# The first pass of a two-layer convolution kernel: image and weights loaded first, the convolutions' tables made later and spread by SyncE, the next image's norm over three units

## The chip, the cores and the metric

The kernel runs on one core of a Trainium2 chip. A core has five engines that work beside one another, each through its own queue in order: TensorE (PE, with its weight loads shown as PEld), VectorE (DVE), ScalarE (ACT), GpSimd (POOL) and SyncE (SP). Transfers are issued by SP, ACT and POOL and run on 16 DMA engines that the core's queues share. The metric is the device time of one execution in microseconds. The time before is the median of three runs, 6082.88 us (6082.45 to 6088.8).

## What is computed

Eight images of 96 x 96 pixels with 192 channels go through two layers; each adds a branch to its input.

```python
# layer 0
x = x + conv0(groupnorm(x))
#   conv0: proj  = x @ W_in + b_in                  (192 -> 384 channels)
#          local = depthwise 3x3 of proj
#          mixed = 0.25 * (four running averages of local) + local
#          out   = layernorm(mixed) @ W_out + b_out (384 -> 192)
# layer 1
x = x + conv1(groupnorm(x))
#   conv1: depthwise 7x7, layernorm, 192 -> 768, gelu, 768 -> 192, * gamma

def groupnorm(v, G=32, eps=1e-5):      # statistics over an image's pixels
    g = v.reshape(B, H, W, G, C // G)  # and the 6 channels of a group
    m = mean(g, axis=(1, 2, 4)); s = var(g, axis=(1, 2, 4))
    return ((g - m) / sqrt(s + eps)).reshape(v.shape)
```

What matters here: the norm of an image needs all its pixels before the first of them can be projected.

## The kernel before

The kernel has five passes, A to E, joined by tensors in DRAM. **A** normalises and projects the image (192 to 384 channels) and stores the result transposed, as `P_d`. **B** reads `P_d` and makes the 3x3 convolution and the running averages with matmuls against banded tables. **C** does the layer norm and the second projection, **D** the 7x7 convolution, **E** the two dense layers. The change touches A and what stands ahead of it.

**Pass A.** An image is cut into 12 units of 8 columns (`WA = 8`, `n_t = 12`), so there are 96 units; unit `u` is unit `t = u % 12` of image `b = u // 12`. Three units make a tile `xq` of 1.77 MB, which three DMAs on SP load (`load_a(n, j)`, L323); six tiles can be held. Tile `n + 6` takes the place of tile `n`; one of its three pieces is asked for in each of the units `3n + 2`, `3n + 3`, `3n + 4`. Within a unit:

- `project_full` (L375): PE multiplies the unit's transposed pixels `xT` by two of the three parts of the weights `win`, into six PSUM banks `pm`.
- `turn_next(0)`, `turn_next(2)` (L361): PE transposes two thirds of the next unit into PSUM tiles `pt`, and ACT writes them to the next `xT` with the norm's factor and shift applied (L368).
- `project_rest` (L388): the third part of the weights; ACT (L401) and DVE (L399) then empty the six banks into `po`.
- `turn_next(1)`: the last third of the next unit, which DVE normalises (L366).
- after each third unit, `store_a` (L408, L421): POOL issues the stores of `po` to `P_d`.

PSUM has two slots for everything that carries the tag `pt`: the transposes and also the small results of the norm.

**The norm of the next image** runs beside this. `stats_a` makes 128 small steps for DVE, 32 channel groups for each of four tiles (`bn_stats`, L330); `share` says how many of them each unit takes, half before the turns and half after. The closing steps are `means` (L49 to L52), `squares` (L57 to L71), `powers` and `shift` (L75 to L79, one power on POOL), `spread` (a matmul, L342) and `keep` (DVE, L352), whose result `cols` the next image's transposes need. They are taken one after another by `end(1)`, `end(1)`, `end(2)` in unit 10 and by `end(1)`, `end(1)` in unit 11. The first image's norm has no unit to hide behind: its statistics and closing steps are written ahead of the loop.

**The convolutions' tables.** Passes B and D multiply by banded matrices that lie in DRAM as `ZB_d` and `Z2_d`. They are made from the small kernels `conv_w` and `dw_kernel`: a loaded copy (`k0`, `k1`), spread over zeros into `z0` and `z1` (L227 to L255; `k1` goes through two PE transposes `kps`, L244), and stored as `Z0_d` and `Z1_d` (L233, L261). From there DRAM-to-DRAM copies lay out shifted rows: three copies of 3.3 MB into `Z2_d` (L269), three of 1.5 MB into `ZB_d` in runs of 128 B (L445) and four small ones for its edges (L455). A zeroed `pad` goes to one row of `X1_d` (L272). The 27 copies that fill `mix` (L211), pass B's mixing matrix, stand ahead of them.

All of this up to L272 is ordered by the compiler and stands at the program's start in a block whose memory is released before pass A's tiles are laid out. The copies of L269 and L272 are issued by ACT, which also loads `win` and the bias (L300, L303). The ones to `ZB_d` are issued by ACT within the loop: `rest_steps` lists 12 stores of zeros to the edges of `P_d` (L434, POOL) and then these seven copies, and from unit 5 on each unit takes one step.

Some small loads and constants of pass C (`wo`, `gb`, `bo`, `mean_w`, `lnb`, L778 to L791) have no predecessors, and the compiler places them among these first instructions too.

Inside `manual_schedule` each engine gets its instructions in the order written.

Of the kernel before, what the change touches and what calls it, by code (L numbers as in the profile page):

```python
# [84 lines left out]
def conv_blocks_kernel(  # L85
# [31 lines left out]
    nc = tc.nc  # L117
# [98 lines left out]

    with (
        tc.tile_pool(name="zprep", bufs=1) as zp,
        tc.tile_pool(name="zpsum", bufs=1, space=PSUM) as zps,
    ):  # L220
        k0 = zp.tile([128, NC, 3, 3], F32, name="k0")
        nc.sync.dma_start(
            k0.rearrange("p m a b -> p m (a b)"),
            conv_w.rearrange("(m p) o a b -> p m (o a b)", p=128),
        )
        z0 = zp.tile([128, NC, 3, ZL], F32, name="z0")
        nc.vector.memset(z0, 0.0)  # L227
        for m in range(NC):
            nc.vector.tensor_copy(
                z0[:, m, :, RB - 1 : RB + 2],  # L230
                k0[:, m],
            )
        nc.sync.dma_start(  # L233
            Z0_d.rearrange("(m p) t l -> p m (t l)", p=128),
            z0.rearrange("p m t l -> p m (t l)"),
        )

        k1 = zp.tile([49, D], F32, name="k1")
        nc.sync.dma_start(k1, dw_kernel.rearrange("a b o c -> (a b) (o c)"))
        kps = zps.tile([128, 512], F32, name="kps")  # L240
        k1t = zp.tile([S, 2, 7, 7], F32, name="k1t")
        for i in range(2):
            half = kps[:S, i * 64 : i * 64 + 49]
            nc.tensor.transpose(half, k1[:, i * S : (i + 1) * S], ident[:49, :49])  # L244
            nc.vector.tensor_copy(k1t[:, i].rearrange("p a b -> p (a b)"), half)
        z1 = zp.tile([S, 2, PH, ZW + 64], F32, name="z1")
        nc.vector.memset(z1, 0.0)
        for i in range(2):
            for p in range(PH):
                for d in range(3):  # L250

                    kw = d * PH + p - 2
                    lo, hi = max(0, -kw), min(PH, 7 - kw)
                    if lo < hi:
                        nc.vector.tensor_copy(  # L255
                            z1[:, i, p, d * ZS + ZO : (d + 1) * ZS].rearrange(
                                "c (t e) -> c t e", e=PH
                            )[:, :, lo:hi],
                            k1t[:, i, :, kw + lo : kw + hi],
                        )  # L260
        nc.sync.dma_start(Z1_d.rearrange("(i c) p l -> c i p l", c=S), z1)  # L261
        for p in range(PH):
            n = -(-(64 - p) // PH)
            src = bass.AP(
                tensor=Z1_d.tensor,
                offset=Z1_d.offset + p * (ZW + 64),
                ap=[[PH * (ZW + 64), D], [PH, n], [1, ZW]],
            )
            nc.scalar.dma_start(Z2_d[p::PH].rearrange("r c l -> c r l"), src)  # L269
        pad = zp.tile([S, D * WV * 2 // S], F32, name="pad")  # L270
        nc.vector.memset(pad, 0.0)
        nc.scalar.dma_start(  # L272
            X1_d[BP * S * PH].rearrange("(i c) v b -> i (c v b)", i=S), pad
        )

# [13 lines left out]
    with ExitStack() as ph:  # L289
# [17 lines left out]
        for i in range(2):  # L307
# [2 lines left out]
                ident[:GROUPS, :GROUPS].unsqueeze(2).to_broadcast([GROUPS, GROUPS, GS]),  # L310
            )
        memberf = member.rearrange("p i g s -> p (i g s)")

        NK = RB // WA
        xq = {}
# [107 lines left out]
                        po[:, :, r, js[0] : js[1]].rearrange("p m j h -> p m (j h)"),  # L423
                    )

        def rest_steps():


            steps = []
            for g in range(NG):  # L430
                for m in range(NC):
                    for row, j in ((RB, 0), (RB + 1, NJ - 1)):
                        steps.append(
                            lambda g=g, m=m, row=row, j=j: nc.gpsimd.dma_start(  # L434
                                P_d[g, m * 128 : (m + 1) * 128, row, :, j], zero
                            )
                        )
            for kh in range(3):
                src = bass.AP(
                    tensor=Z0_d.tensor,  # L440
                    offset=Z0_d.offset + kh * ZL + 1,
                    ap=[[3 * ZL, C], [1, RB], [1, RB]],
                )
                steps.append(
                    lambda kh=kh, src=src: nc.scalar.dma_start(  # L445
                        ZB_d[:RB, :, kh].rearrange("r c o -> c r o"), src
                    )
                )
            for row in range(RB, RB + 4):
                src = bass.AP(  # L450
                    tensor=Z0_d.tensor,
                    offset=Z0_d.offset + (row % 2) * (RB + 1),
                    ap=[[3 * ZL, C], [ZL, 3], [1, RB]],
                )
                steps.append(lambda row=row, src=src: nc.scalar.dma_start(ZB_d[row], src))  # L455
            return steps

        n_t = S // WA
        n_x = B * NK
        rest = rest_steps()  # L460
# [853 lines left out]
```

## Time and profile before

| | before |
|---|---|
| profiled execution, device time | 6083.09 us |
| its span | 6081.0 us |
| granted PE clock, mean | 0.971 |
| PE busy | 5685.5 us, 93% |
| DVE busy | 3456.3 us, 57% |
| ACT busy | 2438.4 us, 40% |
| POOL busy | 2632.8 us, 43% |
| DMA | 1054.36 MB, 173 GB/s over the span |

The page's second part cuts the span in 40 slices of 152 us; a digit is the busy share of a slice in tenths. Pass A fills the first five and a half of them:

```profile
PE   4899989999998999999777759999999999999999
DVE  5455539999996667777632334444444444444442
PEclk9899989999999999999888879999999999999999
DMA  8987669999997888888799962222222222222221
```

The text of the prediction gives times from the start of the span, which is 2 us shorter than the device time. "POOL", "SPq" and "ACTq" with a DMA operation are rows of issuing: the time in which the engine is held by the issue, not the transfer.

### The profile page before, as it was taken

Reading aid. Unit: us, or ns where it says so; the run is one execution under the profiler, and the core shown is the slowest. Engines: PE = TensorE matmul, PEld = TensorE weight load, DVE = VectorE, ACT = ScalarE, POOL = GpSimd, SP = SyncE. Lnnn points to the kernel's source line nnn. Section 1 sums busy time; section 2 is a strip of 40 time slices with the busy share of each in tenths; the row PEclk is TensorE's granted clock in tenths of the full one; section 3 lists DMA queues with packets and bytes.
Section 4 is the critical chain, followed back from the end, with each engine's and each line's share of the span. In section 5 each row is a group of like instructions: output and inputs, shape, how many; then the busy total and the mean of one; then the engine's idle time right before and its main releaser. Section 6 shows DMA issues by size and latency. Waiting matters only on the chain.

```text
span 6081.0 us, 122820 instructions
## 1 busy us (share of the span) xinstructions
PE 5685.5 (93%) x48550; PEld 3948.3 (65%) x48550; DVE 3456.3 (57%) x8026; ACT 2438.4 (40%) x6146; POOL 2632.8 (43%) x2832
## 2 busy tenths in 40 slices
PE   4899989999998999999777759999999999999999
PEld 2455543333335989898666647777777777777777
DVE  5455539999996667777632334444444444444442
ACT  2344447777775555555433322222222222222221
POOL 0111128888886666666544433222222222322222
PEclk9899989999999999999888879999999999999999
DMA  8987669999997888888799962222222222222221
GB/s 238 230 246 238 210 191 244 245 245 242 244 244 203 253 261 267 262 265 263 230 287 286 291 167 78 63 78 62 78 62 77 63 78 63 78 63 78 63 63 37
DMA packets 570206, 1054.36 MB, mean 173 GB/s; under 512 B 109575, under 2 KB 426260, under 8 KB 567328
## 3 DMA queue, kind: packets, MB, share of 16 engines
q1 hardware_dynamic: 385312, 577.65, 35.9%
q0 software_dynamic: 124160, 450.67, 23.9%
q10 hardware_dynamic: 60160, 18.20, 1.5%
q8 instruction: 384, 6.29, 0.5%
q14 instruction: 190, 1.56, 0.1%
HBM read 585.19 MB, written 476.57 MB: 175 GB/s over the span
## 4 chain that ended last, share of the span: by engine, by line
PE 75%; DMA 7%; DVE 1%; issue 1%; POOL 1%; SPq 1%; ACT 0%; POOLq 0%; DVEq 0%; ACTq 0%
PE po L1213 19%; PE po L830 13%; PE hp L1183 12%; PE pl L576 10%; PE hp L1193 7%; PE pa L597 4%; PE pt L828 4%; DMA xin<-X_d 4%; PE pt L1166 2%; PE pa L600 2%; DMA Y_d<-yo 2%; PE py L1021 1%; DMA band<-Z_d 1%; DVE xin L1006 0%; SPq L1060 0%
## 5 line engine op out<-in xcount | busy, mean ns | idle before, releaser
L1202 ACT ACTIVATE g<-hp,b0g 128x384 f32<-128x384 f32 x1152 | 573.9, 580 | 1856.3 <-PE hp L1193 1856.3
L1213 PE MATMUL po<-w1g,g 128*128 128x192 f32 x6912 | 1178.3, 327 | 0.0
L1213 PEld LDWEIGHTS po<-w1g,g 128*128 128x128 f32 x6912 | 1116.6, 190 | 1.6 <-issue 1.1
L830 PE MATMUL po<-wc,mt 128*96 128x193 f32 x4608 | 913.3, 334 | 0.0
L1170 DVE COPY yT<-pt 128x384 f32<-128x384 f32 x288 | 251.4, 873 | 1126.9 <-PE pt L1166 1126.6
L1231 POOL DMA_DIRECT2D out_dram<-xo x576 | 321.2, 560 | 1148.0 <-DVE xo L1220 1119.5
L1183 PE MATMUL hp<-yT,w0w 128*128 128x384 f32 x2304 | 794.5, 488 | 0.4 <-ACT g L1202 0.4
L830 PEld LDWEIGHTS po<-wc,mt 128*96 128x96 f32 x4608 | 702.3, 163 | 68.4 <-ACT mean L834 65.0
L576 PE MATMUL pl<-pin,band 34*32 34x380 f32 (+1 forms) x13824 | 628.6, 489 | 18.5 <-DMA pin<-P_d 18.5
L1183 PEld LDWEIGHTS hp<-yT,w0w 128*128 128x128 f32 x2304 | 431.5, 191 | 231.5 <-issue 2.8
L606 DVE TENSOR_TENSOR_SCAN z<-decay,loc 128x768 f32<-128x768 f32 x288 | 505.8, 1756 | 59.1 <-ACT loc L585 29.3
L1021 PE MATMUL py<-xin,band 63*64 63x248 f32 (+1 forms) x6912 | 405.9, 393 | 141.6 <-DVE xin L1006 139.6
L646 POOL TENSOR_TENSOR mo<-mo,z 128x768 f32<-128x768 f32 x288 | 529.4, 1839 | 3.4 <-ACT mo L601 0.4
L615 DVE TENSOR_TENSOR_SCAN z<-decay,z 128x768 f32<-128x768 f32 x288 | 498.1, 1730 | 0.0
L576 PEld LDWEIGHTS pl<-pin,band 34*32 34x32 f32 x13824 | 233.1, 107 | 396.1 <-issue 394.8
L1021 PEld LDWEIGHTS py<-xin,band 63*64 63x64 f32 x6912 | 343.4, 142 | 203.7 <-DVE xin L1006 125.6
L837 ACT ACTIVATE sq<-pt,mean 96x384 f32<-96x384 f32 x768 | 442.9, 577 | 25.9 <-ACT mean L834 1.0
L1193 PE MATMUL hp<-yT,w0w 64*128 64x384 f32 x2304 | 449.5, 508 | 0.0
L597 PE MATMUL pa<-loc,mix 128*32 128x384 f32 x3456 | 431.9, 493 | 0.0
L600 PE MATMUL pa<-last,down 96*32 96x384 f32 x1152 | 426.8, 493 | 0.9 <-ACT mo L601 0.9
L29 POOL TENSOR_TENSOR rs<-rs_ve,neg_half 96x8 f32<-96x8 f32 x96 | 158.6, 1652 | 607.1 <-DVE rs_ve L28 607.1
L375 PE MATMUL pm<-xT,win 128*128 128x384 f32 x1152 | 401.5, 500 | 20.0 <-ACT xT L368 19.7
(116 smaller groups left out, 7712.8 us busy)
## 6 DMA issues: line engine op xcount, KB each, us to landing
P_d<-po POOLq DMA_DIRECT2D x96, 1152.0 KB, 8.8
pin<-P_d SPq DMA_DIRECT2D x192, 576.0 KB
mt<-M_d SPq DMA_DIRECT2D x576, 192.0 KB
xq<-in_x_dram SPq DMA_DIRECT2D x96, 576.0 KB
xr<-in_x_dram SPq DMA_DIRECT2D x384, 144.0 KB
X_d<-x1u POOLq DMA_DIRECT2D x192, 288.0 KB, 4.1
X_d<-x1c SPq DMA_DIRECT2D x192, 288.0 KB
y<-Y_d SPq DMA_DIRECT2D x24, 2304.0 KB
```

What stands on the lines that cost most here:

```text
L576: nc.tensor.matmul(pls[g][at * RB : (at + 1) * RB, :, lo:hi], band[rows, c, kh, :], pin[rows, c, :, NJ - 1 - j, lo + kh - 1 : hi + kh - 1] ...
L597: nc.tensor.matmul(pa[at], mix[:, i, at], loc[:, q], start=True, stop=True)
L600: nc.tensor.matmul(pa[at], down[:, to], last[:, q], start=True, stop=True)
L606: nc.vector.tensor_tensor_scan(zf, decay_f, loc.rearrange("p q n -> p (q n)"), 0.0, ALU.mult, ALU.add)
L615: nc.vector.tensor_tensor_scan(zr, decay_f, zr, 0.0, ALU.mult, ALU.add)
L646: nc.gpsimd.tensor_tensor(m, m, z, ALU.add)
L830: nc.tensor.matmul(po[:S, b], lhs[m], wc[:, m], start=(m == 0), stop=(m == NC - 1))
L1021: nc.tensor.matmul(pys[t // 2][g][k * 64 : (k + 1) * 64, t % 2, :, lo:hi], pair[k][0][rows, c, d * ZS : d * ZS + 64], pair[k][1][rows, t, ...
L1183: nc.tensor.matmul(hps[m, q], w0w[:, 2 * q, m * 128 : (m + 1) * 128], yT[:, 2 * q], start=True, stop=False,)
L1193: nc.tensor.matmul(hps[m, q], w0w[p, 1, m * 128 : (m + 1) * 128], yT[p, 1], start=False, stop=True,)
L1202: nc.scalar.activation(g[:, m, q], hps[m, q], AF.Gelu, bias=b0g[:, m : m + 1], scale=1.0)
L1213: nc.tensor.matmul(po[:, q], g[:, m, q, k * 128 : (k + 1) * 128], w1g[:, m], start=(m == 0), stop=(m == NE - 1),)
```

## The change

- **Start.** The table-making block ahead of pass A goes. SP first loads the 18 pieces of six tiles, then `k0` and `k1` (`load_kernels`). The table tiles `k0`, `k1`, `z0`, `z1`, `k1t`, `pad` now lie in a pool of pass A.
- **Tables.** In unit 3 `spread_kernels` fills `z0` and `z1`; their zeros are written by POOL instead of DVE, and `kps` takes one of the two `pt` slots. In unit 4 `store_kernels` stores `z0`, `z1` and `pad` from SP. The large copies follow from SP instead of ACT, one at a time: `Z2_d` in units 21, 33 and 45, `ZB_d` in units 57, 69 and 81, its edges in units 84 to 87. The zeros for `P_d` stay on POOL in units 5 to 16. `mix` is filled in units 17 to 19, nine copies in each.
- **Loads.** All three pieces of tile `n + 6` are asked for in unit `3n + 2`.
- **Norm.** `share` gives units 3 to 8 sixteen statistics each, so that they end with unit 8. `ends` places `means` in unit 9, `squares`, `powers` and `shift` in unit 10, `spread` and `keep` in unit 11.

In the program as built, pass C's small loads stand in SP's queue behind the three stores of `store_kernels`, and its constants `mean_w` and `lnb` in DVE's queue within units 3 and 4: `mean_w` ahead of unit 3's evictions, with a wait for the stores of `z0`, `z1` and `pad`, `lnb` ahead of unit 4's, with a wait for `gb`. ACT's table load stands behind a wait for DVE.

```diff
-    for i in range(NJ):
-        for k, (ck, jk) in enumerate(place[i]):
-            for n, (cn, jn) in enumerate(place[i]):
-                if ck == cn < CC - 1:
-                    nc.vector.tensor_copy(
-                        mix[k * RB : (k + 1) * RB, i, n * RB : (n + 1) * RB],
-                        down[jk * RB : (jk + 1) * RB, jn * RB : (jn + 1) * RB],
-                    )
-    with (
-        tc.tile_pool(name="zprep", bufs=1) as zp,
-        tc.tile_pool(name="zpsum", bufs=1, space=PSUM) as zps,
-    ):
...
-        nc.vector.memset(z0, 0.0)
...
-        for p in range(PH):
...
-            nc.scalar.dma_start(Z2_d[p::PH].rearrange("r c l -> c r l"), src)
...
+        zp = ph.enter_context(tc.tile_pool(name="zprep", bufs=1))
...
+        def load_kernels():
+            nc.sync.dma_start(
+                k0.rearrange("p m a b -> p m (a b)"),
+                conv_w.rearrange("(m p) o a b -> p m (o a b)", p=128),
+            )
+            nc.sync.dma_start(k1, dw_kernel.rearrange("a b o c -> (a b) (o c)"))
+
+        def spread_kernels():
+            nc.gpsimd.memset(z0, 0.0)
+            for m in range(NC):
+                nc.vector.tensor_copy(
+                    z0[:, m, :, RB - 1 : RB + 2],
+                    k0[:, m],
+                )
+            kps = ps_t.tile([128, 512], F32, tag="pt", name="kps")
+            for i in range(2):
+                half = kps[:S, i * 64 : i * 64 + 49]
+                nc.tensor.transpose(half, k1[:, i * S : (i + 1) * S], ident[:49, :49])
+                nc.vector.tensor_copy(k1t[:, i].rearrange("p a b -> p (a b)"), half)
+            nc.gpsimd.memset(z1, 0.0)
...
+            nc.gpsimd.memset(pad, 0.0)
+
+        def store_kernels():
+            nc.sync.dma_start(
+                Z0_d.rearrange("(m p) t l -> p m (t l)", p=128),
+                z0.rearrange("p m t l -> p m (t l)"),
+            )
+
+            nc.sync.dma_start(Z1_d.rearrange("(i c) p l -> c i p l", c=S), z1)
+            nc.sync.dma_start(
+                X1_d[BP * S * PH].rearrange("(i c) v b -> i (c v b)", i=S), pad
+            )
...
-        share = (11, 11, 10, 16, 16, 11, 11, 10, 16, 16, 0, 0)
+        rest = {3: spread_kernels, 4: store_kernels}
+        rest |= {5 + i: lambda i=i: zero_edge(i) for i in range(2 * NG * NC)}
+        rest |= {17 + i: lambda i=i: fill_mix(i) for i in range(NJ)}
+        rest |= {21 + 12 * p: lambda p=p: rows_1(p) for p in range(PH)}
+        rest |= {57 + 12 * p: lambda p=p: rows_0(p) for p in range(3)}
+        rest |= {84 + i: lambda i=i: rows_edge(i) for i in range(4)}
+
+        share = (11, 11, 10, 16, 16, 16, 16, 16, 16, 0, 0, 0)
+        ends = {(9, 0): 1, (10, 0): 1, (10, 1): 2, (11, 0): 2}
...
-            for n in range(6):
+            for n in range(NK):
                 for j in range(NJ):
                     load_a(n, j)
+            for n in range(NK, 6):
+                for j in range(NJ):
+                    load_a(n, j)
+            load_kernels()
             bn, last, cols = stats_a(0)
...
-                    if u >= 2 and n + 6 < n_x:
-                        load_a(n + 6, j)
+                    if j == 0 and n + 6 < n_x:
+                        for j in range(NJ):
+                            load_a(n + 6, j)
...
-                    if u >= 5 and rest:
-                        rest.pop(0)()
+                    if u in rest:
+                        rest[u]()
...
-                    def end(n):
-                        if more and t >= n_t - 2:
-                            for _ in range(n):
+                    def end(i):
+                        if more:
+                            for _ in range(ends.get((t, i), 0)):
                                 last.pop(0)()
...
-                    end(1)
+                    end(0)
                     ahead(share[t] // 2)
-                    if t == n_t - 1:
-                        end(1)
                     turn_next(0)
                     turn_next(2)
                     project_rest(cur, pms, po, j)
-                    if t < n_t - 1:
-                        end(1)
+                    end(1)
                     ahead(share[t] - share[t] // 2)
                     turn_next(1)
-                    if t < n_t - 1:
-                        end(2)
```

Here `rows_1`, `rows_0` and `rows_edge` are the old copies into `Z2_d` and `ZB_d` with `nc.sync` in place of `nc.scalar`, `zero_edge` is the old store of zeros, and `fill_mix(i)` is one third of the old loop over `mix`.

More of the change, by code (lines that the diff above doesn't have):

```diff
@@ L206, in conv_blocks_kernel @@
     )
-    for i in range(NJ):
-        for k, (ck, jk) in enumerate(place[i]):
-            for n, (cn, jn) in enumerate(place[i]):
-                if ck == cn < CC - 1:
-                    nc.vector.tensor_copy(
-                        mix[k * RB : (k + 1) * RB, i, n * RB : (n + 1) * RB],
-                        down[jk * RB : (jk + 1) * RB, jn * RB : (jn + 1) * RB],
-                    )
-    with (
-        tc.tile_pool(name="zprep", bufs=1) as zp,
-        tc.tile_pool(name="zpsum", bufs=1, space=PSUM) as zps,
-    ):
[L221 to L226, printed above, removed]
-        nc.vector.memset(z0, 0.0)
[L228 to L248, printed above, removed]
-            for p in range(PH):
[L250 to L268, printed above, removed]
-            nc.scalar.dma_start(Z2_d[p::PH].rearrange("r c l -> c r l"), src)
[L270 to L274, printed above, removed]
@@ L312, in conv_blocks_kernel @@
         memberf = member.rearrange("p i g s -> p (i g s)")
+        k0 = zp.tile([128, NC, 3, 3], F32, name="k0")
+        k1 = zp.tile([49, D], F32, name="k1")
+        z0 = zp.tile([128, NC, 3, ZL], F32, name="z0")
+        z1 = zp.tile([S, 2, PH, ZW + 64], F32, name="z1")
+        k1t = zp.tile([S, 2, 7, 7], F32, name="k1t")
+        pad = zp.tile([S, D * WV * 2 // S], F32, name="pad")
+        def load_kernels():
[17 more added lines that the diff above has]
+            nc.gpsimd.memset(z1, 0.0)
+            for i in range(2):
+                for p in range(PH):
+                    for d in range(3):
+                        kw = d * PH + p - 2
+                        lo, hi = max(0, -kw), min(PH, 7 - kw)
+                        if lo < hi:
+                            nc.vector.tensor_copy(
+                                z1[:, i, p, d * ZS + ZO : (d + 1) * ZS].rearrange(
+                                    "c (t e) -> c t e", e=PH
+                                )[:, :, lo:hi],
+                                k1t[:, i, :, kw + lo : kw + hi],
+                            )
[8 more added lines that the diff above has]
+                X1_d[BP * S * PH].rearrange("(i c) v b -> i (c v b)", i=S), pad
+            )
         NK = RB // WA
@@ L424, in store_a @@
                     )
[L426 to L436, printed above, removed]
-                        )
[L438 to L456, printed above, removed]
@@ new lines, in zero_edge, with fill_mix @@
+        def zero_edge(i):
+            g, m, e = i // (2 * NC), i // 2 % NC, i % 2
+            nc.gpsimd.dma_start(
+                P_d[g, m * 128 : (m + 1) * 128, RB + e, :, e * (NJ - 1)], zero
+            )
+        def fill_mix(i):
+            for k, (ck, jk) in enumerate(place[i]):
+                for n, (cn, jn) in enumerate(place[i]):
+                    if ck == cn < CC - 1:
+                        nc.vector.tensor_copy(
+                            mix[k * RB : (k + 1) * RB, i, n * RB : (n + 1) * RB],
+                            down[jk * RB : (jk + 1) * RB, jn * RB : (jn + 1) * RB],
+                        )
@@ new lines, in rows_1, with rows_0 @@
+        def rows_1(p):
+            n = -(-(64 - p) // PH)
+            src = bass.AP(
+                tensor=Z1_d.tensor,
+                offset=Z1_d.offset + p * (ZW + 64),
+                ap=[[PH * (ZW + 64), D], [PH, n], [1, ZW]],
+            )
+            nc.sync.dma_start(Z2_d[p::PH].rearrange("r c l -> c r l"), src)
+        def rows_0(kh):
+            src = bass.AP(
+                tensor=Z0_d.tensor,
+                offset=Z0_d.offset + kh * ZL + 1,
+                ap=[[3 * ZL, C], [1, RB], [1, RB]],
+            )
+            nc.sync.dma_start(ZB_d[:RB, :, kh].rearrange("r c o -> c r o"), src)
@@ L458, in conv_blocks_kernel, with rows_edge @@
+        def rows_edge(i):
+            src = bass.AP(
+                tensor=Z0_d.tensor,
+                offset=Z0_d.offset + (i % 2) * (RB + 1),
+                ap=[[3 * ZL, C], [ZL, 3], [1, RB]],
+            )
+            nc.sync.dma_start(ZB_d[RB + i], src)
         n_t = S // WA
         n_x = B * NK
-        rest = rest_steps()
-        share = (11, 11, 10, 16, 16, 11, 11, 10, 16, 16, 0, 0)
+        rest = {3: spread_kernels, 4: store_kernels}
+        rest |= {5 + i: lambda i=i: zero_edge(i) for i in range(2 * NG * NC)}
```

## The prediction

> **What bounds the kernel now.** I read the page first: 93% of the span TensorE (PE) is busy, so a change of the first pass can bring only what PE waits for in that pass. The first pass ends where the chain of waits reaches the first convolution matmul (866.28 us). Then I read the timeline up to that point: the start, the PE rows, the DMA issues of ScalarE (ACT).
>
> The timeline's columns are start, length, engine, line, operation, and in brackets the idle time before it with what ended it. The start:
>
> ```profile
> 15.61 109.08 SPq L323 DMA_DIRECT2D xq<-in_x_dram  x24
> 27.44 6.80 DVE L330 BATCH_NORM_STATS2 gn_st<-xq 96x6 f32<-96x144 f32 x32 [11.38 <-DMA xq<-in_x_dram]
> ...
> 49.10 6.80 DVE L330 BATCH_NORM_STATS2 gn_st<-xq 96x6 f32<-96x144 f32 x32 [0.48 <-issue]
> ...
> 69.89 12.79 ACTq L300 DMA_DIRECT2D win<-in_L_conv_W_in_dram  x4
> ...
> 83.26 1.28 ACT L368 ACT_TABLE_LOAD   x1 [83.26 <-DMA win<-in_L_conv_W_in_dram]
> ...
> 85.28 6.15 PE L375 MATMUL pm<-xT,win 128*128 128x384 f32 x12 [19.73 <-ACT xT L368]
> ```
>
> The statistics of image 0 end at 55.9 us, but PE projects only from 85.28: ACT's queue holds the weight loads behind the copies of the second convolution's table (L269, 15.58 to 63.65), and its first activation stands behind them.
>
> From there a unit (8 columns of an image; 96 units) has a fixed beat of 7.18 us in which PE is full:
>
> ```profile
> 300.00:400.00 100.00, 96.47 (x491) 58.75 (x488) 54.62 (x185) 43.32 (x82) 16.09 (x19) 1.00 0.79 240
> ```
>
> (columns: window, length, busy us of PE, weight loads, DVE, ACT, POOL, then granted PE clock, DMA share, GB/s). Where L375 starts later than one beat after its predecessor, time is lost. This happens at each image's end and once between 223 and 280 us:
>
> ```profile
> 159.14 4.06 PE L375 MATMUL pm<-xT,win 128*128 128x384 f32 x12
> ...
> 164.78 0.55 PE L361 MATMUL pt<-ident,xq 96*128 96x96 f32 x4 [0.81 <-ACT xT L368]
> ...
> 170.19 0.20 PE L71 MATMUL gn_ps<-avg,gn_ds 96*32 96x1 f32 x2 [2.72 <-DVE gn_ds L69]
> ...
> 170.71 5.76 PE L375 MATMUL pm<-xT,win 128*128 128x384 f32 x12
> ...
> 180.48 4.06 PE L375 MATMUL pm<-xT,win 128*128 128x384 f32 x12
> ```
>
> ```profile
> 223.54 4.06 PE L375 MATMUL pm<-xT,win 128*128 128x384 f32 x12
> ...
> 243.16 0.90 PE L361 MATMUL pt<-ident,xq 96*128 96x96 f32 x4 [12.76 <-ACT xT L368]
> 244.20 6.90 PE L375 MATMUL pm<-xT,win 128*128 128x384 f32 x12
> ...
> 270.02 0.90 PE L361 MATMUL pt<-ident,xq 96*128 96x96 f32 x4 [8.95 <-ACT xT L368]
> ```
>
> ```profile
> 223.31 19.01 ACTq L445 DMA_DIRECT2D ZB_d<-Z_d  x1
> ...
> 253.97 15.20 ACTq L455 DMA_DIRECT2D ZB_d<-Z_d  x1
> ```
>
> The last two views belong together: ACT is held 19.0 and 15.2 us inside a DMA issue, so it evicts nothing and PE stops. The first pass is therefore 85.3 of start + 96 x 7.18 (less 1 for the last unit, which turns nothing) + 73.0 of lost beats = 846.3, and 20.0 to the first convolution, which the change leaves alone. The 73.0, from the starts of all 96 L375 groups, are 2.1 in the first unit (cold), 43.6 in seven image ends, 27.3 between 223 and 280.
>
> **Part 1, the start: gains 37.** SP now begins with the image instead of six small loads and two stores; ACT begins with the weights. Tile 0 took 11.8 us from its first issue (15.61 to 27.44) with the table copies beside it; without them, 2 us of latency and 1.77 + 0.59 MB (weights) at the 309 GB/s which the windows show for 20 to 25 us make an estimated 9.6. Then four groups of 32 statistics: 28.5 us at the pace of loads (27.44 to 55.90), 27.2 if the data is there. With a first issue at 0.7, statistics end between 37.5 and 41.0; I take 39.5. From their end to the column factors is 6.7 us in the trace (55.90 to 62.61); ACT's table load (1.28) now stands behind those factors, as it waits for a DVE event in the new queue; 0.72 passes from activation to L375. So PE starts at 39.5 + 8.7 = 48.2 instead of 85.3: **-37.1** (ends -35.6 and -40.4, the latter if the table load hides).
>
> **Part 2, image ends: gain 20.** Each end costs, over two units, 7.0, 7.1, 5.3, 6.8, 5.3, 6.8, 5.3. The cheap kind is 4.38 + 0.90: 0.81 for a second transpose that needs the one free PSUM slot, 2.72 for DVE's chain of the squares, 0.85 of the small matmuls, 0.90 for the spread. With the steps over units 9, 10 and 11 the squares run during the full projection of unit 10: DVE reaches them about 1.2 us into the unit, they take 2.3 (167.92 to 170.05), PE is occupied for 3.9. So 2.72 goes, and a second slot wait of 0.81 comes, since the slot of the sums is then held in two units: 0.85 + 2 x 0.81 + 0.90 = 3.4, with bounds 2.6 and 5. The dearer kind is the clock: after the stall L375 took 5.76 us for 4.06. Here a rule can be weighed. In the Trainium skill, "TensorE: Matmul & The Clock Gate", the section on the HAM gate, an idle stretch of some 3.4 us halves the clock, judged in free-running windows. The trace has 0.81 + 2.72 of idling and a slow group in four of seven ends, which fits windows that hit or miss. By the rule, two waits of 0.8 a unit apart never do it, and every end costs 3.4; were each new wait as bad as the trace's dear ends (1.2 to 1.7 more), the gain would be 19.8 - 7 x 1.5 = 9. The rule's length decides, as no 0.8 us wait in the trace (image 2's) slowed a group. 43.6 - 7 x 3.4 = **-19.8**. Statistics of 16 a unit in units 3 to 8 are what units 3, 4, 8 and 9 had before, at the full beat, so they cost nothing.
>
> **Part 3, ACT's DMA issues: gain 27.** All seven table DMAs of L445/L455 go to SP and with them the 27.3 lost between 223 and 280. What SP holds behind them are the image loads. Three tables of 3.3 MB now follow the tile loaded at units 20, 32, 44; three of 12,288 packets of 128 B at 56, 68, 80. The next tile is asked for at unit 11 of the image and needed at unit 3 of the next: 28.7 us of cover. The rule that speaks against it: "DMA: Bandwidth & Descriptors", the section on queues, rings and completion order, says that each of SP and ACT owns one ring on the same engines, and a ring is consumed in order. The tables ran beside the image on another ring; in SP's they hold the tile up. By the rule, if table and tile were asked for together, a tile would wait 25 us (the first 128 B table, 216.13 to 242.3) and take 7 itself: 3 late, six times, +20. By the rows the table starts earlier: nothing on SP holds it, so it goes out right behind the tile of unit 8, some 20 us before the next request, and three 3.3 MB copies took only 48 us with four tiles beside them (16 each). It is over about when the tile is asked for, so the cover holds: **-27.3**, and nothing paid; I follow the rows and leave the 20 to a rival. P_d stores landed within 14.2 us in that same window; their buffer is needed after 26. The four edge DMAs come at units 84 to 87, when no tile is left to load. L434's zeros stay on POOL at the same units. The 27 mix copies (3.2 us of DVE) go into units 5 to 7 of image 1, 1.06 each, where DVE waited 2.1 us for PE before the eviction.
>
> **Part 4, the tables' making: pays 8.** At unit 3 it lands amid the beat. POOL first issues the stores of unit 2 (2.82 + 0.75 in the trace, from 0.2 before the unit), then clears z0: POOL cleared 384 columns in 0.42, so 594 in an estimated 0.65 and z1's 1632 in 1.75. DVE's z0 copies wait for this (4.0 us into the unit), the k1t copy behind them, and the second kps transpose waits for k1t, as it did at 6.45 us. It stands ahead of the projection in PE's queue: some 4.5 us of idle PE, long enough for a slow L375 (1.2 to 1.7 more). DVE fills z1 (22 copies, about 2 us), and then meets mean_w's memset: pass C's work shares memory with z0, z1 and pad in the new layout and waits for their stores, about 14 us into the unit beside the P_d stores; behind it are this unit's evictions, for which the next unit's second pair of matmuls waits, 1 to 2 us. lnb waits for gb in the same way. **+8**; ends 4.5 (only the transpose) and 16 (stores that land like the slowest P_d store, gb too).
>
> **Sum.** -37.1 - 19.8 - 27.3 + 8 = -76.2 on the profiled execution's 6083.1, which agrees with the median of 6082.9: **6007**. Nothing after 866 us changes but its start.
>
> **Rivals.** (A) DVE's waits at units 3 to 5 are the cost that decides: stores and gb land late, twice, each with a slow clock: 24 instead of 8, **6023**. For it: two DMA waits at the head of an in-order DVE queue. (B) The shared ring bites a little: tables plus stores saturate the DMA engines (share 0.97 in 200 to 300 us), and each of six tables holds a tile or a store for 5 us: **6037**. Against: no store there landed late. (C) The slower side: each table occupies SP's ring so long that DVE's statistics stop and PE with them. A table queued 1 us or so into ACT's 25 us kind is harmless; at 48 us each, what all three took together, the tile of unit 11 lands about 13 us too late, six times 13 = 78 eats everything; from there it decides. At 55 us it is 20 each: **6127**. Against: no trace row is near 48 for one. (D) The moved loads do not come sooner, as the weights or a DMA wait still set the start, 15 us of part 1 lost: **6022**.
>
> **Chances.** Forecast 0.62, within 5997 to 6017; A 0.13, B 0.11, D 0.06; better than 5997 0.04; C 0.03; next to nothing left 0.01. Range 5990 to 6037, with some 0.1 outside, most of it above. 0.2% is 12 us, what a measurement can tell from no change; the cases give faster 0.96, same 0.01, slower 0.03.
>
> **What would show it.** First L375 near 48 us; seven image ends without a wait of L71 on DVE; no ACT DMA issue after the weights; a unit 3 with PE idle before the second kps matmul and DVE idle before mean_w; no statistics waiting for xq after image 0; first convolution near 790. It is wrong if statistics wait for xq at units 3 to 7 of images 2 to 7, if the first tile needs more than 12 us, or if unit 3 loses over 16.

## The result

| | before | after |
|---|---|---|
| median of the runs | 6082.66 us (4 runs, 6079.82 to 6088.8) | 6014.85 us (4 runs, 6011.68 to 6029.3) |
| profiled execution | 6083.09 us | 6011.68 us |
| first L375 (L362 after) | 85.28 us | 50.09 us |
| last L375 (L362 after) | 840.11 us | 771.78 us |
| first long run of convolution matmuls | 866.28 us | 797.95 us |

The ratio is 0.9892, with a 95% interval of 0.9874 to 0.9909: 1.1% faster, 67.8 us by the medians. 68.3 us of it is seen inside pass A. What lies behind pass A takes 5240.9 us before and 5238.1 after (span less the start of the last L375 group), a difference smaller than the spread of one kernel's runs (6079.82 to 6088.8).

The page of the changed kernel, the same four rows of its second part as shown before:

```profile
PE   6999989999998999999677769999999999999999
DVE  5555469999995667777532334444444444444442
PEclk9999989999999999999888889999999999999999
DMA  7999779999987888888899952222222222222221
```

The first slices show the gain: PE is busy for 6 tenths of the first slice instead of 4, and for 9 of the second instead of 8. The other digits that differ come of the rest having moved left.

The start, from the timeline of the changed kernel (start, length, engine, line, operation, idle before and its releaser):

```profile
0.73 28.64 SPq L310 DMA_DIRECT2D xq<-in_x_dram  x18
...
11.56 6.80 DVE L317 BATCH_NORM_STATS2 gn_st<-xq 96x6 f32<-96x144 f32 x32 [8.42 <-DMA xq<-in_x_dram]
...
33.86 6.80 DVE L317 BATCH_NORM_STATS2 gn_st<-xq 96x6 f32<-96x144 f32 x32 [1.01 <-DMA xq<-in_x_dram]
...
47.43 1.28 ACT L355 ACT_TABLE_LOAD   x1 [47.43 <-DVE cols L339]
...
50.09 5.18 PE L362 MATMUL pm<-xT,win 128*128 128x384 f32 x12
```

The image comes first; the last tile's statistics wait 1.01 us for data, so the loads set the pace; ACT's table load stands on the path behind the column factors.

An image's end, from PE's timeline:

```profile
128.65 4.06 PE L362 MATMUL pm<-xT,win 128*128 128x384 f32 x12
...
134.29 0.55 PE L348 MATMUL pt<-ident,xq 96*128 96x96 f32 x4 [0.81 <-ACT xT L355]
...
137.29 4.06 PE L362 MATMUL pm<-xT,win 128*128 128x384 f32 x12
141.29 0.22 PE L71 MATMUL gn_ps<-avg,gn_ds 96*32 96x1 f32 x2
...
142.80 0.55 PE L348 MATMUL pt<-ident,xq 96*128 96x96 f32 x4 [0.81 <-ACT xT L355]
...
145.80 4.06 PE L362 MATMUL pm<-xT,win 128*128 128x384 f32 x12
```

L71 no longer waits for DVE; a second wait of 0.81 us for a PSUM slot has come. No group is longer than 4.06 us (granted clock 1.00 from 128 to 154 us). The beats are 8.64, 8.51 and 8.08, so the three units lose 1.46 + 1.33 + 0.90 = 3.7 us over 7.18 each, and so does each of the seven ends to 0.02 us. No beat is lost anywhere else behind unit 5; a window that holds an image's end has PE busy for 98.4 of 100 us:

```profile
300.00:400.00 100.00, 98.38 (x496) 59.68 (x493) 58.42 (x204) 44.02 (x82) 14.78 (x18) 1.00 0.92 273
```

Before, the same window held an image's end too (its unit 10 starts at 372.84 us) and showed 96.47: the 3.53 us of idle PE there are the waits of 0.81 and 2.72, the 1.62 now are twice 0.81. So the beat is full outside the ends in both kernels. The busy share counts the modelled ends of matmuls, so the beats say more than this number.

The new loss is at units 3 and 4. PE's timeline, and DVE's of the same stretch:

```profile
77.20 0.31 PE L272 MATMUL kps<-ident,k 49*96 49x49 f32 x1 [4.12 <-DVE k1t L273]
77.44 6.91 PE L362 MATMUL pm<-xT,win 128*128 128x384 f32 x12
87.46 1.48 PE L362 MATMUL pm<-xT,win 128*128 128x384 f32 x4
92.29 4.53 PE L362 MATMUL pm<-xT,win 128*128 128x384 f32 x8 [3.34 <-DVE po L386]
99.94 4.06 PE L362 MATMUL pm<-xT,win 128*128 128x384 f32 x12
```

```profile
76.73 0.30 DVE L265 COPY z<-k 128x9 f32<-128x9 f32 x3 [2.15 <-POOL z L263]
...
91.64 0.17 DVE L789 MEMSET mean_w<- 128x128 f32 x1 [10.32 <-DMA X_d<-pad]
91.72 1.04 DVE L386 TENSOR_SCALAR po<-pm,bin__126 128x384 f32<-128x384 f32 x2
```

Unit 3 starts 4.7 us late behind kps, unit 4 another 2.8 late as unit 3's projection takes 6.91 us (granted clock 0.57 from 77 to 84 us), and unit 5 another 5.3, since DVE stands 10.3 us before mean_w with unit 3's evictions behind it. Together 12.8 us.

### The profile page after: what moved, and what is told of

The parts are those of the page before. It is cut to its first block, busy times and chain, and to the rows that moved or that the text cites. A ratio compares the mean times of both kernels' runs of the same rounds, so it can differ in the third digit from the quotient of the medians.

```text
span 6009.9 us, 122810 instructions
## 1 busy us (share of the span) xinstructions
PE 5680.5 (95%) x48550; PEld 3943.4 (66%) x48550; DVE 3454.0 (57%) x8023; ACT 2440.3 (41%) x6146; POOL 2634.7 (44%) x2835
## 4 chain that ended last, share of the span: by engine, by line
PE 77%; DMA 6%; DVE 1%; issue 1%; SPq 1%; POOL 1%; ACT 0%; DVEq 0%; POOLq 0%; ACTq 0%
PE po L1216 19%; PE po L833 13%; PE hp L1186 12%; PE pl L579 10%; PE hp L1196 7%; PE pa L600 5%; PE pt L831 4%; DMA xin<-X_d 4%; PE py L1024 2%; PE pt L1169 2%; PE pa L603 2%; DMA Y_d<-yo 1%; DVE xin L1009 1%; DMA band<-Z_d 0%; SPq L1063 0%
## 5 line engine op out<-in xcount | busy, mean ns | idle before, releaser
L362 PE MATMUL pm<-xT,win 128*128 128x384 f32 x1152 | 395.9, 494 | 3.3 <-DVE po L386 3.3
```

## Experiments

Single times scatter by several us, as the passes behind A do not repeat exactly: from the start of the last projection to the end of the span they take 5237 to 5245 us in all kernels here but one (5251). So the experiments are read from the profile of each run, by the start of pass A's first and last L375 group and by the beats between them. "Units 3, 4" is the time over 7.18 us a unit that the tables' making costs, up to the start of unit 6; "ends" is the same over the seven image ends.

| kernel | time, us | first | last | units 3, 4 | ends |
|---|---|---|---|---|---|
| before | 6082.66 | 85.28 | 840.11 | 0 | 43.6 |
| after | 6014.85 | 50.09 | 771.78 | 12.8 | 25.9 |
| e1 constants on POOL | 6009.82 | 49.03 | 765.61 | 6.4 | 25.9 |
| e2 zeros first | 6015.40 | 48.83 | 773.15 | 14.2 | 25.9 |
| e3 both | 6001.17 | 49.60 | 761.67 | 2.5 | 25.9 |
| e4 tables from ACT, spaced | 6016.02 | 49.68 | 773.13 | 13.7 | 25.9 |
| e5 tables from SP, packed | 6039.00 | 49.19 | 785.43 | 13.8 | 25.9 |
| e6 before, weights first | 6094.73 | 101.94 | 855.54 | 0 | 43.6 |
| e7 norm in two units | 6037.27 | 50.66 | 791.66 | 13.8 | 43.4 |
| e8 e3, slots freed | 5988.37 | 49.29 | 747.00 | 2.5 | 10.8 |
| e9 before, copies later | 6070.68 | 63.63 | 828.22 | 0 | 51.8 |
| e10 e8, tables early | 5991.17 | 50.62 | 744.24 | 0 | 10.8 |
| e11 before, tables spaced | 6067.64 | 84.88 | 820.31 | 0 | 51.4 |

After and e10 are medians of four and five runs, before of four; the others are single runs. That a tile's three pieces are now asked for in one unit was not tested by itself; before, e9 and e11, which ask for one piece a unit, lose no beat to late tiles behind the start either.

**Units 3 and 4: e1, e2, e3.** e1 moves two constants of pass C to POOL:

```diff
-            nc.vector.memset(mean_w, 1.0 / C)
+            nc.gpsimd.memset(mean_w, 1.0 / C)
...
-                nc.vector.tensor_copy(lnb[:, m], gb[:, 1, m : m + 1].to_broadcast([128, S]))
+                nc.gpsimd.tensor_copy(lnb[:, m], gb[:, 1, m : m + 1].to_broadcast([128, S]))
```

> Pass C's constants mean_w and lnb are written by POOL instead of DVE, so their waits for the stores of z0, z1 and pad and for gb no longer stand ahead of evictions in DVE's queue; the table-making stays as it is. In the changed kernel units 3 and 4 lost 4.70 (kps), 2.84 and 5.30 us, 12.8 in all. Theory 1 (two separate waits: PE waits for k1t in unit 3, then DVE waits for the stores in unit 4): 5.3 goes, 7.5 stays, pass A ends near 766.5 instead of 771.8. Theory 2 (all of it is the one late start of table-making, and mean_w only fills time that is lost anyway): under 1 us goes.

The loss fell from 12.8 to 6.4 (7.5 was expected): unit 5 no longer starts late. e2 moves the three memsets of zeros into `load_kernels`, ahead of the first norm:

```diff
+            for z in (z0, z1, pad):
+                nc.gpsimd.memset(z, 0.0)
...
-            nc.gpsimd.memset(z0, 0.0)
...
-            nc.gpsimd.memset(z1, 0.0)
...
-            nc.gpsimd.memset(pad, 0.0)
```

> The zeros of z0, z1 and pad are written by POOL before the first image's norm instead of in unit 3; mean_w and lnb stay on DVE. Theory 1 (two waits in series on a fixed arrival: the stores land about 91 us whatever PE does): the kps stall of 4.2 us and the slow matmuls behind it go (7.5 us), but unit 4 comes earlier and DVE still waits for the stores of z1 and pad, which land only some 2.5 us earlier, so that most of the gain is lost again: net gain 2 to 4 us. Theory 2 (the waits are independent): net gain 7.5, unit 4's 5.3 unchanged.

It gained nothing: 14.2 us are lost, where the changed kernel loses 12.8, and e4, e5 and e7, which leave this part as it is, 13.7 to 13.8. Rows of PE and DVE from the timeline of e2:

```profile
82.39 1.48 PE L361 MATMUL pm<-xT,win 128*128 128x384 f32 x4
92.12 0.17 DVE L788 MEMSET mean_w<- 128x128 f32 x1 [13.58 <-DMA X_d<-pad]
...
92.77 5.42 PE L361 MATMUL pm<-xT,win 128*128 128x384 f32 x8 [8.90 <-DVE po L385]
```

Unit 4 began 5.1 us sooner than in the changed kernel, and mean_w, behind pad's store, came at 92.1, no sooner than there (91.6), although SP had issued that store 2.7 us earlier (77.37 against 80.12). PE's wait grew from 3.34 to 8.90 us. e3 has both edits:

> Both edits: zeros first, mean_w and lnb on POOL. Theory 1: all 12.8 us of units 3 and 4 go but for about 1 (the two kps transposes and DVE's 22 copies), pass A's last projection starts near 760 instead of 771.8, more than the two single gains together. Theory 2: the sum of the single gains, no more.

2.5 us of loss are left, where the effects of the two single runs added up (6.4 less, 1.4 more) would leave 7.8. So there are two waits in series, and the second ends at a time that the first does not move: the landing of pad's store. What sets that time can be read from two traces. In the changed kernel unit 2's output (3.7 MB, issued from 72.5 us on POOL) goes out ahead of it and lands between 78.7 and 88.1. In e10 below SP issues pad's store at 69.0, ahead of this output, and its wait ends at 78.2. Taking away the first wait alone is worth nothing. Theory 1 holds, and more strongly than the expectation for e2 had it.

**The tables' DMAs: e4, e5, e11.** e4 gives the tables back to ACT in the changed kernel's units (three times `nc.scalar.dma_start` for `nc.sync.dma_start` in `rows_1`, `rows_0`, `rows_edge`).

> The ten table copies stay in the units where the changed kernel has them, but are issued by ACT as before. Theory of the prediction (it is the engine that counts: ACT is held in the issue and cannot evict): each of the three 128-byte tables holds ACT for 9 to 19 us, and pass A ends 20 to 27 us later than 771.8. Rival (it is the spacing: an issue holds its engine only while an earlier table is still draining): every issue takes under 1 us, no beat is lost, and pass A ends within 2 us of 771.8, or a little over where the four edge copies follow one another.

ACT's issues of the three 128-byte tables, from its timeline in e4:

```profile
489.06 0.54 ACTq L444 DMA_DIRECT2D ZB_d<-Z_d  x1
578.89 0.54 ACTq L444 DMA_DIRECT2D ZB_d<-Z_d  x1
668.72 0.54 ACTq L444 DMA_DIRECT2D ZB_d<-Z_d  x1
```

0.54 us each, where the kernel before shows 19.01 for the second; no beat is lost from unit 6 on but in the image ends, and pass A ends 1.4 us later than in the changed kernel, within the rival's 2. The rival holds: ACT was held before because a table followed another that was still draining. e11 tests it from the other side, in the kernel before:

```diff
-                    if u >= 5 and rest:
+                    if rest and (5 <= u < 17 or u in (57, 69, 81) or u >= 84):
                         rest.pop(0)()
```

> The kernel before, with only the seven copies into ZB_d spread over units 57, 69, 81 and 84 to 87, still issued by ACT; all else as before. Theory now (spacing alone makes the gain): the 27.3 us lost between 223 and 280 us go, pass A's last L375 starts near 812.8 instead of 840.1, no ACT issue over 1 us but in the four edge copies. Theory of the prediction (the engine): at least half of the 27 stays.

All 27.3 us between 223 and 280 are gone, with ACT as the issuer. Pass A ended only 19.8 us sooner (820.3, not the 812.8 expected), because the image ends cost 51.4 instead of 43.6: rows of one of them, from PE's timeline in e11:

```profile
350.77 0.55 PE L361 MATMUL pt<-ident,xq 96*128 96x96 f32 x4 [0.81 <-ACT xT L368]
...
356.17 0.24 PE L71 MATMUL gn_ps<-avg,gn_ds 96*32 96x1 f32 x2 [2.72 <-DVE gn_ds L69]
...
357.03 6.71 PE L375 MATMUL pm<-xT,win 128*128 128x384 f32 x12
```

The waits are those of before, 0.81 and 2.72; behind them a slow group (5.2 to 6.8 us for 4.06) now comes in all seven ends instead of four. Here it took 6.71 us, with a granted clock of 0.55 from 357 to 363 us. e5 keeps SP as the issuer and packs the tables:

```diff
-        rest |= {21 + 12 * p: lambda p=p: rows_1(p) for p in range(PH)}
-        rest |= {57 + 12 * p: lambda p=p: rows_0(p) for p in range(3)}
-        rest |= {84 + i: lambda i=i: rows_edge(i) for i in range(4)}
+        rest |= {57 + 12 * p: lambda p=p: rows_1(p) for p in range(PH)}
+        rest |= {20 + p: lambda p=p: rows_0(p) for p in range(3)}
+        rest |= {23 + i: lambda i=i: rows_edge(i) for i in range(4)}
```

> SP still issues the tables, but the three 128-byte tables follow one another in units 20 to 22 and the four edge copies in units 23 to 26, as close as in the kernel before; the 3.3 MB tables go to units 57, 69 and 81. Theory now (spacing keeps the issue short; the engine only decides who is held): SP is held some 19 and 9 us, as ACT was, and the tile asked for in unit 23 goes out up to 25 us late against 28.7 us of cover, so PE loses 0 to 5 us; pass A ends between 771 and 777. Rival C of the prediction (a tile behind tables in SP's ring starves the statistics): waits of the statistics for xq in units 27 to 31 of image 2 and 15 us or more lost. Rival 2 (packed tables stall whatever issues them, as they saturate the DMA engines): about 27 us lost, pass A ends near 799.

SP's issues and the statistics that follow, from the timelines of SP and DVE in e5:

```profile
213.96 38.63 SPq L444 DMA_DIRECT2D ZB_d<-Z_d  x3
252.70 18.41 SPq L310 DMA_DIRECT2D xq<-in_x_dram  x3
...
283.02 1.77 DVE L317 BATCH_NORM_STATS2 gn_st<-xq 96x6 f32<-96x144 f32 x8 [14.76 <-DMA xq<-in_x_dram]
```

SP stands 38.6 us in three tables; a tile that unit 23 asks for (about 238) is issued between 252.7 and 271.1, its statistics in unit 27 wait 14.8 us, and unit 28 loses 12.5 us of beat. Pass A ends 13.7 us later than in the changed kernel; the rest lies in the start and in units 0 to 5. The expectation (0 to 5) was too mild: the cover of 28.7 us was overrun. So of the 27.3 us that packed tables cost on ACT, SP's slack hides about half; spacing alone hides all.

**The start: e6, e9.** e6 moves only the weights ahead of the table block of the kernel before:

```diff
+    win_pool = ExitStack()
+    wcp = win_pool.enter_context(tc.tile_pool(name="win_pool", bufs=1))
+    win = wcp.tile([128, 3, C], F32, name="win")
+    for p, k, c in spans:
+        nc.scalar.dma_start(win[p, k], W_in[c])
...
     with (
         tc.tile_pool(name="zprep", bufs=1) as zp,
```

> The kernel before, with only the loads of win and the bias moved ahead of the table-making block (a pool of their own); image loads, tables and norm as before. Theory of the prediction: in the kernel before ACT's late weights alone set the start, behind them the image's statistics end at 55.9, so the first L375 moves from 85.3 to about 64 to 66 us, 19 to 21 us sooner; the other 14 to 16 us of the change's start come from the image's loads. Rival (the weights' transfer matters little, ACT is held by its table copies until about 64 and its activations come after): the first L375 near 66 all the same, but with ACT as the releaser; a larger loss, first L375 at 75 or later, if the weights now delay the image.

Neither reason came true: the start is 16.7 us later than before, and what delayed the image was not the weights. SP's and DVE's rows from the timelines of e6:

```profile
30.02 0.31 SPq L326 DMA_DIRECT2D xq<-in_x_dram  x1
69.82 5.29 SPq L326 DMA_DIRECT2D xq<-in_x_dram  x4
85.69 6.80 DVE L333 BATCH_NORM_STATS2 gn_st<-xq 96x6 f32<-96x144 f32 x32 [34.03 <-DMA xq<-in_x_dram]
```

Between 30 and 70 us SP issues nothing. In these traces the DMAs of SP and ACT take turns on eight completion semaphores (the counters that tell of a landing), and each issue first waits for the DMA that last had its semaphore. The fourth tile's first piece came to share one with the second 3.3 MB copy (issued at 18.6 us), and the trace puts down its wait of 39.5 us to that copy. In the kernel before a stop of the same kind (41.72 to 82.72 in SP's timeline) fell on the fifth tile, which nobody needed yet. e9 takes the three copies from the start of the kernel before instead:

```diff
-            nc.scalar.dma_start(Z2_d[p::PH].rearrange("r c l -> c r l"), src)
...
+                    if u in (45, 57, 69):
+                        rows_1((u - 45) // 12)
```

> The kernel before, with only the three 3.3 MB copies (L269) taken from the start and issued by ACT in units 45, 57 and 69. In the run with only the weights moved the fourth image tile came 34 us late: its issue on SP stood behind a wait for a semaphore that a table copy had taken. Theory now (the copies hold the start twice, ACT's queue ahead of the weights and, by the shared DMA semaphores, SP's ahead of image tiles): without them the weights are there before the statistics end at about 56, no tile comes late, and the first L375 is at 64 to 66 us instead of 85.3; the image loads moved ahead of small loads and stores give the other 14 to 16. Rival (the copies are not what holds the start): first L375 above 75.

From the timeline of e9:

```profile
15.68 2.31 ACTq L292 DMA_DIRECT2D win<-in_L_conv_W_in_dram  x4
...
60.98 1.28 ACT L360 ACT_TABLE_LOAD   x1 [60.98 <-DVE cols L344]
...
63.63 5.85 PE L367 MATMUL pm<-xT,win 128*128 128x384 f32 x12
```

The copies held the start: without them it is 63.6, 21.7 us sooner, just ahead of the 64 to 66 expected. The other 13.5 are what is left for the image's loads ahead of everything (first issue at 0.73 instead of 15.6 us); no run has that edit alone. e9's total gain is small because its image ends are all of the dear kind (51.8), as in e11, and the stall of the packed tables costs 1.9 us more than before.

**The norm: e7, e8.** e7 puts the closing steps back into units 10 and 11 (with `end` in its old places), and the old `share`:

```diff
-        share = (11, 11, 10, 16, 16, 16, 16, 16, 16, 0, 0, 0)
-        ends = {(9, 0): 1, (10, 0): 1, (10, 1): 2, (11, 0): 2}
+        share = (11, 11, 10, 16, 16, 11, 11, 10, 16, 16, 0, 0)
+        ends = {(10, 0): 1, (10, 1): 1, (10, 2): 2, (11, 0): 1, (11, 1): 1}
...
```

> The changed kernel with the norm's closing steps back in units 10 and 11 and the old shares of statistics; start and tables as changed. Theory: the seven image ends cost 5.3 to 7.0 each again instead of 3.70, with L71 waiting 2.7 us for DVE, and pass A ends 11 to 18 us later than 771.8 (783 to 790), the dear ends those in which the following L375 group is slow. Rival (in the kernel before the ends were dear because of the crowding of loads or of DMA issues, not because of the two units): under 5 us lost.

The ends cost 43.4 again, 17.5 more; the rest of the 19.9 us is 0.6 of start, 0.8 in the first unit and 1.0 in units 3 and 4, which puts the end (791.7) just past the 783 to 790 expected. e8 goes on from e3: the matmuls of `means` and `squares` become steps of their own and stand at the end of units 9 and 10.

```diff
...
-        ends = {(9, 0): 1, (10, 0): 1, (10, 1): 2, (11, 0): 2}
+        ends = {(9, 0): 1, (9, 1): 1, (10, 0): 1, (10, 1): 3, (11, 0): 2}
```

> On top of zeros first and constants on POOL: the matmuls of the sums and of the squares are taken apart from their DVE steps and placed at the end of units 9 and 10, so that their PSUM slot is not held while two transposes of that unit need one. Theory (each image end has two slot waits of 0.8 us for ACT): 1.47 and 1.33 fall to 0.6 and 0.5 or less, 3.70 to about 2.1, seven times: pass A ends 11 us sooner than the run with both edits (761.7), near 750.5. Rival (the waits come back elsewhere, as DVE reaches the squares later or the sums wait at the unit's end): under 4 us.

PE's timeline in e8, the same place as shown above for the changed kernel:

```profile
118.97 4.06 PE L375 MATMUL pm<-xT,win 128*128 128x384 f32 x12
122.87 0.83 PE L361 MATMUL pt<-ident,xq 96*128 96x96 f32 x8
...
126.64 4.06 PE L375 MATMUL pm<-xT,win 128*128 128x384 f32 x12
130.54 0.83 PE L361 MATMUL pt<-ident,xq 96*128 96x96 f32 x8
...
133.97 4.06 PE L375 MATMUL pm<-xT,win 128*128 128x384 f32 x12
```

The eight transposes run in one piece, with no wait of 0.81; an end costs 0.49 + 0.15 + 0.90 = 1.5 us instead of 3.7, and pass A ends 14.7 us sooner than in e3 (11 were expected).

**The version that beats both: e10.** On top of e8, `load_kernels` and `spread_kernels` stand ahead of the first statistics, where DVE waits for the image anyway, and one activation of a constant makes ACT load its table early:

```diff
+            load_kernels()
             for n in range(NK):
...
-            load_kernels()
+            warm = sp.tile([128, 1], F32, tag="warm", name="warm")
+            nc.scalar.activation(
+                warm, neg_half[:, 0:1], AF.Identity, bias=neg_half[:, 0:1], scale=1.0
+            )
+            spread_kernels()
```

> On top of the run with free slots: the small kernels are loaded ahead of the image and spread by DVE before the first statistics, and one small activation at the start makes ACT load its table early. Theory: unit 3 loses nothing (2.4 before), the table load (1.28) leaves the path to the first projection, the first image tile comes about 1 us later: pass A's last projection starts 2 to 3 us sooner than 747.0, the time is near 5986, 1.6% under the kernel before. Rival (the two small loads hold the image's loads by more than they bring): 747 or later.

Pass A ends 2.8 us sooner than in e8, though not as thought. Unit 3's 2.4 are gone, but the first projection comes at 50.62, 1.3 later: the first tile's statistics start 2.1 us later than in e8 (13.29 for 11.24), and the table load's leaving the path brought 0.65 of its 1.28. The first unit lost less (1.0 for 2.6). Its ratio to before is 0.9847 (0.9832 to 0.9862), median 5991.17.

## Why the prediction was right, and where it was not

**In total** -76.2 us was forecast against the profiled execution, which showed -71.4: -68.3 in pass A, 3 behind it. The forecast 6007 lies 5 us under the profiled execution and 8 under the median. Parts 1, 2 and 4 fell short by 1.9, 2.1 and 4.8 us, all the same way; 1.0 saved in the first unit and the 3 behind pass A, neither of them forecast, brought the total closer than its parts.

**Part 1, the start.** -37.1 forecast, -35.2 measured. The statistics ended at 40.7 instead of 39.5: the windows from 10 to 40 us of the changed kernel show 245 to 270 GB/s with the DMA engines full, and not the 309 taken from a window in which DRAM copies ran too. The chain behind (8.7) took 9.4, the table load being in it as forecast. e9 and e6 show that the prediction saw one of two holds of the start before: the copies stand in ACT's queue, and they also keep semaphores for which SP's loads wait.

**Part 2, image ends.** -19.8 forecast, -17.7 measured. L71's wait went and a second slot wait of 0.81 came, both as stated; the term mis-sized is the remainder, 0.66 + 0.52 for the small matmuls in units 9 and 10 where 0.85 was taken. (DVE's squares took 2.1 us, 167.92 to 170.05, and not the 2.3 that the text puts beside these times; nothing hangs on it.) That the dear ends are slow through the clock, the rows confirm: granted clock 0.76 from 170 to 177 us before, 0.55 in e11's end. The Trainium skill, "TensorE: Matmul & The Clock Gate" (the HAM gate), and the rows agree that waits of 0.81 a unit apart cost no clock: not one slow group in the 35 ends of after, e1, e2, e4 and e5. That this also takes away a cost that differs from build to build (43.6, 51.4, 51.8 for the same waits) was not foreseen.

**Part 3, ACT's DMA issues.** -27.3 forecast, and all 27.3 gone. The amount is right and the reason is not: the step "All seven table DMAs of L445/L455 go to SP and with them the 27.3" took the engine for the cause. e4 and e11 lose no beat with ACT as the issuer once the tables are a dozen units apart; e5 loses 12.5 with SP when they are not. That the number came out was luck in this: the edit that moved the tables to SP also spread them. The trace of the kernel before had a row that says so, the first table's issue, and the prediction read only the 19.01 of the second:

```profile
216.13 0.59 ACTq L445 DMA_DIRECT2D ZB_d<-Z_d  x1
```

The tiles' cover held, but not because a table "is over about when the tile is asked for". The 48 us behind the estimate of 16 a copy are the time that ACT stood in the issues; the third copy's landing was still waited for at 82.3. In the changed kernel a copy of 3.3 MB took 31 to 33 us to land (212.8 to 245.6 for the first, by its semaphore). The tile asked for at 235.8 stood 10 us beside it and landed at 252.8, 12 us ahead of its unit (265.2). The rule it weighed ("DMA: Bandwidth & Descriptors", queues, rings and completion order: a ring is consumed in order) agrees with e5, where a tile's first issue behind tables lasted 15.4 us. Rival C's way of losing time is seen there too, 12.5 us once where C had 13 to 20 at each of six tables, and only where tables are packed.

**Part 4, units 3 and 4.** +8 forecast, +12.8 measured. The kps wait (4.1 us for 4.5 forecast) was right. Mis-sized were the slow projection behind kps, 2.8 for 1.2 to 1.7, and what mean_w costs, 5.3 for 1 to 2. The stores landed later than thought: counted as the prediction counts, from where unit 3 starts at full beat (72.7 us, so that z0's copies at 76.73 are its 4.0), mean_w came at 18.9 us for about 14. So PE waits 3.34, and its next eight matmuls are slow too (4.53, where twelve take 4.06; granted clock 0.66 from 92 to 97 us). This is rival A's mechanism at a third of its extra price; gb cost nothing here, lnb's copies came without a wait.

Rival D did not occur: the weights are there early. Rival B neither: the shares of the DMA engines reach 0.97 (480 to 570 us) and no store or tile was late enough to cost a beat.

## What to carry to other kernels

Look at the first DMA issue of a row of them as well as at the longest: if the first is short, spreading them out frees whichever engine issues them, and moving them to another engine only chooses who stands still. Before a wait is removed, find the next one behind it and what sets its end; if that is a transfer's landing that the edit does not move, removing the first wait alone brings nothing. When work is moved into a loop, see what the compiler places behind it: constants of a later pass came to wait for the moved tables' stores, and that wait stood at the head of a queue that the beat needs.

## What the runs showed of the hardware

Issuing a copy of 12,288 runs of 128 B held ACT or SP 0.5 to 0.7 us when no other table was on its way, and longer when one was: 19.0 and 9.4 us on ACT in the kernel before, 24.6 and 13.3 us on SP in e5.

After the same two waits of PE, 0.81 and 2.72 us with 2.7 us of matmuls between them, the next unit lost 0.9 to 3.7 us of beat, by whether its first group took 4.06, 5.2 to 5.8 or 6.7 to 6.9 us. Four of seven groups were slow in before, e6 and e7, seven of seven in e9 and e11; what decides it is not shown.

The wait for pad's store (48 KB) ended at 91.5 to 92.5 us in four builds (after, e1, e2, e3) that issued it between 77.4 and 80.4 behind 3.7 MB of larger stores: 3 us of earlier issue did not make it land earlier. Issued at 69.0, ahead of them (e10), it landed at 78.2.
